# A written-out order of 2,640 steps in a transformer kernel, replaced by another order of the same steps

## The chip, the core and the metric

The kernel runs on one core of a Trainium2 chip. Its time is the time of one execution on the device, in microseconds (us). A profile is one execution recorded by the hardware profiler. Its engines are TensorE (PE, with weight loads shown apart as PEld), VectorE (DVE), ScalarE (ACT), GpSimd (POOL) and SyncE (SP), which here only issues transfers (DMAs). Each engine works through its own list of instructions in order, and waits on semaphores for what the others produce.

## The reference

For 16 batch elements of 256 tokens with 256 features, in float32: an attention of x to a context y with RMS norms (layer 0), then a decoder block on its result: causal self-attention with rotary embedding (layer 1), cross-attention to the same y with rotary embedding (layer 2), and an MLP with 1,024 hidden features. Every attention has 16 heads of 16 features. Cut to what matters:

```python
# layer 0
Q = rmsnorm(x) @ Wq; K = rmsnorm(y) @ Wk; V = rmsnorm(y) @ Wv
x = rmsnorm(x + softmax(Q K^T * scale) V @ Wo)
# layer 1
h = ln(x); q, k, v = h @ sa_wq, h @ sa_wk, h @ sa_wv
x = x + causal_attention(rope(q), rope(k), v) @ sa_wo
# layer 2
h = ln(x); q, k, v = h @ ca_wq, y @ ca_wk, y @ ca_wv
x = x + attention(rope(q), rope(k), v) @ ca_wo
# MLP
x = x + gelu(ln(x) @ fc1_w) @ fc2_w
```

## The kernel before, in words

There are 48 attentions, 16 batch elements in each of three layers. ORDER gives the layer of each of the 48 in the order in which they run; the number of an attention (0 to 47) is its place there. Class Att holds the parts of one attention as methods, and most of them are generators: each `yield` ends a segment whose instructions go to one engine (or to one engine's DMA queue). PLAN, a long string written out by hand, says in which order the segments of all attentions are called: each word, such as `q.18` or `scores.16.2`, runs the next segment of that generator (`step`). The instructions are issued in just this order, so PLAN fixes the order on every engine and in every queue. The MLP follows in a loop of its own; only a few words `mlp...` at the end of PLAN belong to it.

The methods, and what their segments are, in the order of the work:

- `stats_x`, `stats_y` (mean squares on VectorE, then the root on GpSimd, L525 and L526), `send` and `receive` (a row of roots through DRAM) for layer 0. `stats`, `norm` (L553, VectorE) for layers 1 and 2. The normed tile is turned either by TensorE (`turn`, copied by ScalarE, L575) or by VectorE in 32 by 32 pieces (`pieces`, L584) and a way through DRAM: the second segment of `pieces` stores (L592, `turn_hop<-bits`), `pieces_in` reads back (L598).
- `q`, `k`, `v`: a dense group of 16 matrix products on TensorE (L633 or L645), then the segments that take it out of PSUM: for layers 1 and 2 a bias addition on ScalarE (L760), a shuffle and two products on VectorE (L768, L774), their sum (L810, L863, L866). `q_high`, `q_low`, `k_high`, `k_low` split the result into two parts for a faster kind of product in layers 0 and 2 (from attention 2 on); `q_out` and `k_out` move them between partitions by DMA (L840, L887).
- `scores.i.n`: block n of the scores of attention i on TensorE (L964 for the fast kind, L953 for the other), then two exponentials on ScalarE (L976), and in layer 1 two masks on GpSimd (L984). `values.i.n`: the product with v (L1007); halfway ScalarE copies the result out (L1022), at the end `take_last` does so on VectorE.
- `heads_in`, `sums_in`, `invert`, `divide`: DMAs (L1030, L1041, L1054, L1060) and VectorE work (L1051, L1067) that divide by the sums. `project`: the output product (L645) and the residual addition (L1080). `finish` ends layer 0. `keep` adds a bias row to the residual on GpSimd (L621).
- `combine`: eight additions and subtractions on GpSimd (L1124, L1135) that prepare sums of weights for the MLP. `load_piece`, `load_later`: loads issued by GpSimd; `load_early`: by SyncE.

Tiles come from pools with few buffers; a segment that takes a tile waits until a former user of that buffer is done. The ones that matter here: the tag `a` (two buffers) holds the biased q or k until its rotation is done, and also the pieces ("bits") until they are stored; `hl` has one buffer, `qm`, `kT` and `av` have two; the PSUM tiles of scores have two sets, the dense ones three, the values one.

Of the kernel before, what the change touches and what calls it, by code (L numbers as in the profile page):

```python
# [54 lines left out]
scores.0.0 scores.0.0 v.0 scores.0.0 scores.0.1 q.1 scores.0.1 scores.0.1 spread.1 spread.1  # L55
scores.0.2 q.1 v.1 v.1 v.0 scores.0.2 v.0 scores.0.2 stats_x.3 values.0.0 values.0.1 stats_x.2
stats_x.3 scores.0.3 v.1 values.0.1 load_piece.5.0 k.1 stats_x.2 scores.0.3 send.2 stats_y.2
scores.0.3 k.2 send.2 k.1 load_piece.5.1
scores.1.0 load_early.4 k_high.2 load_early.0 k_low.2 q.2 scores.1.0 send.3 receive.2 scores.1.0
values.0.2 load_early.3 send.3 scores.1.1 q.3 scores.1.1 q.2 scores.1.1 values.0.3 k_out.2  # L60
q_high.2 scores.1.2 take_last.0 q_low.2 v.2 v.2 stats_y.2 scores.1.2 receive.3 q_low.2 stats_y.3
scores.1.2 q_out.2 values.1.0 stats_y.6 load_piece.6.1 scores.1.3 sums_in.0 stats_y.3 stats_x.6
k.3 scores.1.3 scores.1.3 load.4 values.1.1 k_high.3
scores.2.0 values.1.1 k_low.3 scores.2.0 values.1.2 q.3 invert.0 values.1.3 scores.2.0 heads_in.0
take_last.1 q_high.3 scores.2.1 invert.0 v.3 k_out.3 q_low.3 scores.2.1 q_low.3 heads_in.0
scores.2.1 v.2 stats_x.4 q_out.3 scores.2.2 k.4 stats_x.4 stats_y.4 sums_in.1 scores.2.2
load_piece.5.2 send.4 scores.2.2 values.2.0 v.3 send.4 divide.0 v.3 k_high.4 scores.2.3 q.4
load_early.2 scores.2.3 invert.0 invert.1 k_low.4 scores.2.3 divide.1 values.2.1 stats_y.4
receive.4 invert.1
scores.3.0 heads_in.1 values.2.1 stats_x.6 fold_of_att scores.3.0 heads_in.1 load_piece.5.3  # L70
values.2.2 divide.0 scores.3.0 q.4 values.2.3 k_out.4 q_high.4 scores.3.1 take_last.2 project.0
q_low.4 scores.3.1 invert.1 q_low.4 scores.3.1 values.3.0 q_out.4 project.0 fold_of_att scores.3.2
project.0 v.4 v.4 load_piece.6.0 scores.3.2 stats_y.8 project.0 scores.3.2 values.3.1 sums_in.2
finish.0 scores.3.3 values.3.1 stats.5 k.6 fold_of_att scores.3.3 v.4 stats.5 scores.3.3
values.3.2 load_later.0 norm.5 k_high.6 divide.1 load_piece.6.2
scores.4.0 heads_in.2 stats_x.8 values.3.3 scores.4.0 turn.5 send.6 send.6 take_last.3 scores.4.0
project.1 fold_of_att fold_of_att turn.5 heads_in.2 k_low.6 scores.4.1 invert.2 project.1 q.5
sums_in.3 scores.4.1 fold_of_att load_early.1 scores.4.1 receive.6 values.4.0 project.1 heads_in.3
q.5 scores.4.2 invert.3 k.5 project.1 invert.2 q.5 scores.4.2 q.5 load_later.1 invert.3 scores.4.2
q.5 values.4.1 load_piece.7.1 q.5 k.5 load_piece.7.0 scores.4.3 q.5 invert.2 values.4.1  # L80
load_piece.7.2 q.6 k.5 q.5 stats_y.6 k.5 scores.4.3 k.5 heads_in.3 v.5 v.5 scores.4.3 divide.2 k.5
load_piece.6.3 q.6 stats_x.8 values.4.2 invert.3 v.5 q_high.6
scores.5.0 divide.3 finish.1 q_low.6 k_out.6 values.4.3 scores.5.0 v.6 take_last.4 scores.5.0
scores.5.0 stats.7 sums_in.4 scores.5.1 divide.2 stats.7 q_low.6 project.2 v.6 scores.5.1 norm.7
scores.5.0 pieces.7 q_out.6 scores.5.1 scores.5.1 values.5.0 project.2 pieces.7 scores.5.2
project.2 scores.5.1 heads_in.4 k.8 send.8 invert.4 scores.5.2 project.2 divide.3 invert.4
scores.5.2 v.6 scores.5.2 values.5.1 finish.2 keep.5 k_high.8
scores.6.0 values.5.1 stats.9 pieces_in.7 project.3 scores.6.0 scores.5.2 k_low.8 stats.9
scores.6.0 values.5.2 heads_in.4 divide.4 norm.9 stats_y.8 project.3 scores.6.1 take_last.5
load_later.9 q.7 scores.6.1 project.3 sums_in.5 load_later.8 scores.6.1 pieces.9 heads_in.5  # L90
values.6.0 stats_y.10 q.7 scores.6.2 pieces.9 k.7 q.7 send.8 scores.6.2 invert.5 q.7 invert.5
scores.6.2 invert.4 q.7 values.6.1 q.7 scores.6.3 receive.8 q.7 k.7 q.8 invert.5 q.7 k.7
values.6.1 pieces_in.9 v.7 v.7 k.7 scores.6.3 load_later.4 k.7 load_piece.7.3 scores.6.3 k.7
heads_in.5 values.6.2 divide.5 q.8 project.3
scores.7.0 divide.4 q_high.8 v.7 k_out.8 project.4 scores.7.0 stats_x.10 scores.7.0 scores.7.0
values.6.3 heads_in.6 load_later.5 scores.7.1 divide.5 scores.7.0 take_last.6 project.5 project.4
scores.7.1 q_low.8 scores.7.1 scores.7.1 q_low.8 v.8 project.5 q_out.8 scores.7.1 stats.11
scores.7.2 sums_in.6 project.4 stats.11 q.9 scores.7.2 load_later.7 norm.11 scores.7.2 finish.3
scores.7.2 values.7.0 heads_in.6 pieces.11 stats_x.10 q.9 values.7.1
scores.8.0 load_piece.8.0 q.9 values.7.1 k.10 pieces.11 scores.7.2 scores.8.0 q.9 v.8 load_later.6  # L100
scores.8.0 send.10 values.7.2 v.8 send.10 stats_y.10 gain_ca k_high.10 q.9 scores.8.1 project.4
k.9 q.9 scores.8.1 keep.7 pieces_in.11 take_last.7 invert.6 scores.8.1 values.8.0 stats_x.14 k.9
invert.6 scores.8.2 q.9 v.9 v.9 k.9 load_piece.9.0 scores.8.2 k_low.10 divide.6 sums_in.7
load_piece.8.1 scores.8.2 k.9 values.8.1 keep.9 k.9 q.9 scores.8.3 values.8.1 invert.6 k.11 v.9
scores.8.3 k.9 heads_in.7 scores.8.3 finish.4 values.8.2 invert.7 receive.10 k.11 heads_in.7
scores.9.0 k.11 values.8.3 invert.7 scores.9.0 k.11 k_out.10 q.10 take_last.8 scores.9.0
scores.9.0 k.11 load_later.10 sums_in.8 scores.9.1 q.10 scores.9.0 stats.13 stats_x.14 q_high.10
v.10 divide.6 v.10 scores.9.1 divide.7 q_low.10 invert.7 stats.13 project.6 scores.9.1 q_low.10
scores.9.1 v.10 q_out.10 scores.9.2 project.6 scores.9.1 heads_in.8 invert.8 q.11 k.11 scores.9.2
load_piece.8.2 heads_in.8 divide.7 scores.9.2 load_piece.9.1 values.9.0 send.14 project.6  # L110
scores.9.2 q.11 invert.8 values.9.1 scores.9.2 k_high.11
scores.10.0 q.11 load_later.3 values.9.1 project.7 norm.13 scores.10.0 k_low.11 scores.10.0 q.11
values.9.2 k_out.11 pieces.13 q.11 scores.10.1 project.7 k.12 scores.10.1 take_last.9 q.11
scores.10.1 invert.8 values.10.0 stats.12 q_high.11 pieces.13 scores.10.2 stats.12 sums_in.9 v.11
q_low.11 scores.10.2 divide.8 norm.12 load_piece.10.0 k.12 heads_in.9 q_low.11 v.11 turn.12
scores.10.2 k.12 values.10.1 q_out.11 stats.16 turn.12 scores.10.3 pieces_in.13 values.10.1 v.11
fold_of_fc1 stats.16 scores.10.3 divide.8 q.12 load_later.2 k.12 scores.10.3 k.12 load_piece.8.3
k.12 values.10.2 q.12 stats_y.14
scores.11.0 fold_of_fc1 k_high.12 project.8 fold_of_fc1 invert.9 scores.11.0 stats_y.14 norm.16
heads_in.9 q.12 scores.11.0 project.6 values.10.3 k_low.12 invert.9 q.12 scores.11.1 q.12 k_out.12  # L120
k.13 scores.11.1 take_last.10 q.12 scores.11.1 heads_in.10 values.11.0 q_high.12 scores.11.2
invert.9 v.12 v.12 divide.9 q_low.12 scores.11.2 keep.11 send.14 q_low.12 scores.11.2 project.8
values.11.1 q_out.12 gain_fc1.0 k.13 scores.11.3 divide.9 k.14 sums_in.10 scores.11.3 v.12
scores.11.3 project.9 pieces.16 keep.12 values.11.1 k.13 k_high.14
scores.12.0 k.13 project.9 values.11.2 scores.12.0 k.13 pieces.16 values.11.3 heads_in.10 stats.15
scores.12.0 take_last.11 heads_in.11 stats.15 scores.12.1 k.13 q.13 receive.14 norm.15 scores.12.1
sums_in.11 invert.10 scores.12.1 k_low.14 divide.10 values.12.0 project.8 invert.10 q.13
scores.12.2 heads_in.11 q.13 values.12.1 scores.12.2 pieces_in.16 q.13 v.13 v.13 scores.12.2 q.13
q.13 values.12.1 invert.10 scores.12.3 q.13 q.13 pieces.15 q.14 scores.12.3 v.13 pieces.15
scores.12.3 k_out.14 values.12.2 q.14  # L130
scores.13.0 divide.10 fold_of_fc1 finish.6 k.15 scores.13.0 pieces_in.15 stats.19 scores.13.0
stats_x.17 scores.13.0 values.12.3 q_high.14 scores.13.1 take_last.12 k.15 invert.11 v.14 v.14
# [216 lines left out]
def xattn_kernel(  # L349
# [1068 lines left out]
    combined = []  # L1418
# [77 lines left out]
    def begin(word):  # L1496
# [3 lines left out]
        if name == "combine":  # L1500
            return combine()
        args = [int(a) for a in args]
# [562 lines left out]
```

## Time and profile before

| | us |
|---|---|
| median of 3 runs (lowest, highest) | 887.47 (886.6, 888.52) |
| the profiled execution's own time | 891.12 |
| its span, first to last instruction | 889.4 |
| TensorE busy | 871.2 |
| VectorE busy | 690.9 |
| ScalarE busy | 570.4 |
| GpSimd busy | 349.3 |

The page gives the busy time of each engine, the span in 40 equal slices (a digit is the busy share in tenths; PEclk is TensorE's granted clock in tenths of full speed), the DMA queues, the chain of waits that ended last and the costliest groups of instructions. A line of the timeline reads: start, length, engine, source line, operation, what it writes and what it reads, shapes, how many instructions, and in brackets the idle time before with what ended it. A TensorE group of 16 matrix products in float32 appears as 32 instructions.

### The profile page before, as it was taken

The numbers are of one execution on the slowest core, as the hardware profiler recorded it, in microseconds if no ns is written. First come the engines' busy times: TensorE is split into PE (matmuls) and PEld (weight loads), VectorE is DVE, ScalarE is ACT, GpSimd is POOL, SyncE is SP. The second block draws the span as 40 slices with busy tenths as digits, with TensorE's granted clock in tenths as the row PEclk, the third lists the DMA queues.
The fourth block names the chain that finished last, engine by engine and source line by source line (L and its number), as shares of the span: only waits on it lengthen the run. The fifth ranks groups of instructions, "written<-read, shape, count | busy, mean of one in ns | idle before, by whom it ended". The sixth has DMA issues, their size and how long they took to land.

```text
span 889.4 us, 32873 instructions
## 1 busy us (share of the span) xinstructions
PE 871.2 (98%) x13762; PEld 559.2 (63%) x13762; DVE 690.9 (78%) x1534; ACT 570.4 (64%) x801; POOL 349.3 (39%) x558
## 2 busy tenths in 40 slices
PE   8999999999999999999999999999999999999997
PEld 4455555555555555555554555555556799999997
DVE  5468789888888889889885888989894677777662
ACT  4787567776686767778756777777875733334440
POOL 3234766517364246175483335345142132221000
PEclk9999999999999999999999999999999999999999
DMA  8666455544444344343434233233431022111201
GB/s 273 208 193 176 147 163 175 178 132 133 134 148 123 110 134 161 117 159 120 155 118 145 84 124 111 87 118 116 158 107 54 17 72 72 57 44 44 72 25 50
DMA packets 101454, 107.04 MB, mean 120 GB/s; under 512 B 26602, under 2 KB 81778, under 8 KB 101298
## 3 DMA queue, kind: packets, MB, share of 16 engines
q1 hardware_dynamic: 96210, 89.89, 30.7%
q0 software_dynamic: 4400, 14.42, 5.7%
q8 instruction: 110, 1.80, 0.9%
q10 hardware_dynamic: 688, 0.54, 0.2%
q14 instruction: 46, 0.38, 0.1%
HBM read 46.33 MB, written 13.65 MB: 67 GB/s over the span
## 4 chain that ended last, share of the span: by engine, by line
PE 79%; DVE 8%; DMA 5%; ACT 2%; issue 2%; SPq 2%; POOL 2%; ACTq 0%; DVEq 0%; POOLq 0%
PE d L633 15%; PE d L645 14%; PE A L1007 14%; PE S L964 7%; PE upX L1221 6%; PE A L1319 6%; PE S L953 5%; PE downZ L1319 3%; PE upZ L1221 3%; PE d L1319 2%; PE d L1221 2%; ACT pt L976 1%; DMA turn_hop<-bits 1%; DMA qm<-qm 1%; DVE xn L553 1%
## 5 line engine op out<-in xcount | busy, mean ns | idle before, releaser
L976 ACT ACTIVATE pt<-S 128x1024 f32<-128x1024 f32 x224 | 217.7, 1023 | 98.9 <-PE S L953 59.4
L1007 PE MATMUL A<-pt,va 128*32 128x256 f32 (+1 forms) x3072 | 184.6, 363 | 2.9 <-ACT av L1022 2.7
L976 ACT ACTIVATE pt<-S,sy 128x1024 f32<-128x1024 f32 x128 | 136.4, 1115 | 35.5 <-PE S L964 26.2
L1007 PEld LDWEIGHTS A<-pt,va 128*32 128x32 f32 x3072 | 94.1, 110 | 68.0 <-issue 7.0
L984 POOL TENSOR_SCALAR_AFFINE_SELECT pt<-pt 128x512 f32<-128x512 f32 x128 | 90.7, 728 | 74.4 <-ACT pt L976 73.9
L964 PEld LDWEIGHTS S<-qm,kT 32*128 32x128 f32 x1920 | 66.9, 183 | 52.2 <-issue 24.2
L964 PE MATMUL S<-qm,kT 32*128 32x256 f32 x1920 | 93.5, 304 | 3.8 <-ACT pt L976 3.4
L621 POOL TENSOR_TENSOR cur<-cur,bias 128x512 f32<-128x512 f32 x48 | 64.8, 1353 | 32.9 <-DVE xn L553 32.7
L525 POOL TENSOR_SCALAR r_ln<-bmv 128x2 f32<-128x2 f32 x48 | 14.4, 300 | 149.6 <-DVE bmv L544 137.4
L953 PE MATMUL S<-qm,kT 32*64 32x512 f32 (+1 forms) x1152 | 63.3, 512 | 1.1 <-DVE kT L866 1.0
L760 ACT ACTIVATE a<-d,qk_bias 128x256 f32<-128x256 f32 x128 | 53.9, 477 | 14.0 <-PE d L633 4.8
L1243 ACT COPY g<-upX 128x512 f32<-128x512 f32 x28 | 15.0, 589 | 72.4 <-issue 68.1
L633 PE MATMUL d<-hT,sa 128*32 128x256 f32 x1024 | 61.4, 382 | 0.0
L553 DVE TENSOR_SCALAR xn<-cur,bmv,r_ln 128x256 f32<-128x256 f32 x96 | 47.5, 543 | 4.2 <-POOL r_ln L526 4.0
L1067 DVE TENSOR_TENSOR oT<-oT,inv 128x512 f32<-128x512 f32 x48 | 38.2, 798 | 15.1 <-DMA rq<-rq_hop 3.7
L774 DVE TENSOR_TENSOR a<-a,turn 128x512 f32<-128x512 f32 x64 | 47.9, 748 | 1.3
L1259 ACT ACTIVATE g<-g,fb 128x256 f32<-128x256 f32 x96 | 41.0, 499 | 11.1 <-DVE g L1248 11.1
L768 DVE STREAM_SHUFFLE u<-a 128x512 f32<-128x512 f32 x64 | 47.5, 743 | 0.4 <-issue 0.4
L774 DVE TENSOR_TENSOR u<-u,turn 128x512 f32<-128x512 f32 x64 | 47.0, 734 | 0.0
L1065 POOL TENSOR_TENSOR seen<-seen,sums 128x64 f32<-128x64 f32 x48 | 20.9, 436 | 62.9 <-DVE sums L1051 59.2
L633 PEld LDWEIGHTS d<-hT,sa 128*32 128x32 f32 x1024 | 30.3, 109 | 24.2 <-issue 3.2
L1022 DVE COPY av<-A 128x512 f32<-128x512 f32 x47 | 32.1, 683 | 13.4 <-PE A L1007 13.4
(176 smaller groups left out, 1701.1 us busy)
## 6 DMA issues: line engine op xcount, KB each, us to landing
kT<-hl SPq DMA_DIRECT2D x60, 256.0 KB
qm<-qm SPq DMA_DIRECT2D x60, 256.0 KB
oT<-av SPq DMA_DIRECT2D x192, 64.0 KB
inv<-inv_hop SPq DMA_DIRECT2D x96, 128.0 KB
turn_hop<-bits SPq DMA_DIRECT2D x33, 256.0 KB
hT<-turn_hop SPq DMA_DIRECT2D x92, 64.0 KB
out<-res SPq DMA_DIRECT2D x15, 256.0 KB
cur<-in_x POOLq DMA_DIRECT2D x11, 256.0 KB, 3.3
```

What stands on the lines that cost most here:

```text
L553: nc.vector.tensor_scalar(xn[:, c, :], src[:, c, :], mv[:, c, 0:1], r[:, c : c + 1], ALU.subtract, ALU.mult,)
L621: nc.gpsimd.tensor_tensor(t, t, bias_sb[:, row : row + D].unsqueeze(1).to_broadcast([P, NC, D]), ALU.add)
L633: nc.tensor.matmul(o, lhsT=w[:, k, at + t * P + j : at + t * P + j + 32], rhs=tokens, start=(k == 0), stop=(k == KC - 1), skip_group_check ...
L645: nc.tensor.matmul(ps[j : j + 32, c * D : (c + 1) * D], lhsT=some_tokens(src, k, c, j), rhs=w[:, k, at : at + D], start=(k == 0), stop=(k ...
L774: nc.vector.tensor_tensor(t, t, table.unsqueeze(1).to_broadcast([P, KC, S]), ALU.mult)
L953: nc.tensor.matmul(ps[64 * half : 64 * half + 64, 2 * m * u : 2 * m * (u + 1)] .rearrange("p (i s) -> p i s", i=2), lhsT=self.kT[r, t, at] ...
L964: nc.tensor.matmul(ps[:, at : at + m], lhsT=self.kd[r, i, t, kc * P : (kc + 1) * P].bitcast(F32R), rhs=self.qd[r, i, h, t, q0:S].bitcast(F ...
L976: nc.scalar.activation(pt[:, :, :w], ps[:, :, :w], AF.Exp, scale=scale)
L984: nc.gpsimd.affine_select(out=diag, in_=diag, compare_op=ALU.is_ge, fill=0.0, base=0, pattern=[[0, 2], [0, 2], [1, P]], channel_multiplier=-1,
L1007: nc.tensor.matmul(self.av[32 * r : 32 * r + 32, i, q0:S], lhsT=self.va[:, kc, 8 * t + 2 * r + i, :], rhs=pts[r // 2][:, r % 2, i * m : (i ...
L1221: nc.tensor.matmul(o if len(b.shape) == 2 else by_groups(o), lhsT=a[:, c * P : (c + 1) * P], rhs=b, start=(first and c % 2 == 0), stop=Tru ...
L1319: nc.tensor.matmul(ps[:, c, :], lhsT=a[f // 2][:, f % 2, c * P : (c + 1) * P], rhs=b[:, f, :], start=(first and c == 0 and f == 0), stop=True,
```

## The change

PLAN is replaced by another order of the same words. `combine` is changed with it: its word's number now chooses between the two generators, where the number was not read before. The PLAN's diff covers nearly all of its lines; here are the places that the prediction speaks of, and the whole change of code:

```diff
...
-load_later.9 q.7 scores.6.1 project.3 sums_in.5 load_later.8 scores.6.1 pieces.9 heads_in.5
-values.6.0 stats_y.10 q.7 scores.6.2 pieces.9 k.7 q.7 send.8 scores.6.2 invert.5 q.7 invert.5
...
-values.15.1 q.16 scores.15.3 invert.14 pieces.19 q.17 scores.15.3 q.16 pieces.19 stats_x.20
-k_out.17 values.15.1 project.13 q.16 project.12 stats_x.20 scores.15.3 q.17 values.15.2 q_high.17
...
-scores.32.0 invert.30 k.33 stats.37 divide.29 values.31.2 invert.30 scores.32.0 norm.35 keep.33
-k.33 send.36 v.33 scores.32.0 k.33 combine.0 take_last.31 scores.32.1 invert.30 norm.37
-load_piece.14.3 q.33 scores.32.1 pieces.35 v.33 divide.30 stats.39 k.33 sums_in.31 scores.32.1
-values.32.0 k.33 combine.2 pieces.35 scores.32.2 q.33 heads_in.30 project.29 keep.37 scores.32.2
...
-scores.46.0 q.47 divide.44 values.45.3 scores.46.0 q.47 project.44 scores.46.0 q.47 q.47 k_high.47
-scores.46.1 q.47 v.47 v.47 take_last.45 scores.46.1 k_low.47 sums_in.45 scores.46.1 mlp.1.stats
-values.46.0 q_high.47 scores.46.2 k_out.47 project.43 q_low.47 scores.46.2 q_low.47 scores.46.2
-mlp.0.norm values.46.1 q_out.47 scores.46.3 invert.45 project.44 invert.45 divide.45 scores.46.3
-mlp.0.keep v.47 mlp.0.turn project.43 heads_in.45 values.46.1 scores.46.3 mlp.0.turn values.46.2
...
+scores.6.1 take_last.5 norm.9 scores.6.1 sums_in.5 values.6.0 pieces.9 q.7 values.6.1 project.3
+pieces.9 invert.4 scores.6.2 q.7 values.6.1 k.7 scores.6.2 q.7 receive.8 load_early.2 invert.5
...
+sums_in.15 k.18 scores.16.1 turn.18 pieces.21 invert.14 scores.16.2 turn.18 send.20 keep.18 v.17
+q.18 pieces.21 scores.16.2 k.18 scores.16.1 scores.16.2 invert.15 stats_y.20 values.16.0 invert.15
+scores.16.2 q.18
...
+scores.31.0 take_last.30 scores.31.0 q_low.32 combine.0 scores.31.1 finish.27 scores.31.0
...
+scores.32.0 values.31.1 invert.30 divide.29 k.33 invert.30 keep.33 values.31.2 scores.32.0 k.33
+send.36 load_piece.14.3 v.33 scores.32.0 k.33 send.34 v.33 take_last.31 stats.35 k.33 invert.30
+scores.32.1 combine.1 k.33 q.33 scores.32.1 stats.39 receive.34 stats.37 scores.32.1 sums_in.31
+values.32.0 divide.30 v.33 q.33 stats_y.34 scores.32.2 norm.35 project.29 scores.32.2 pieces.35
...
+scores.33.0 keep.35 pieces.37 invert.31 k.34 q_low.34 scores.33.0 receive.36 project.30
...
+scores.33.1 values.33.0 k.35 scores.33.2 combine.2 k.35 heads_in.32 project.31 invert.32
...
+values.33.2 pieces_in.37 keep.37 v.34 q.35 scores.34.1 take_last.33 v.35 v.35 combine.4
...
+scores.46.1 k_low.47 values.46.0 divide.44 q_high.47 k_out.47 scores.46.2 values.46.1 q_low.47
+scores.46.2 q_low.47 project.44 scores.46.2 v.47 q_out.47 invert.45 divide.43 invert.45
+scores.46.3 project.44 project.43 scores.46.3 mlp.0.norm values.46.1 scores.46.3 mlp.1.stats
+mlp.0.keep values.46.2 heads_in.45
...
-    def combine():
+    def combine(n):
...
-            combined.extend([*[combine_down()] * 4, *[combine_up()] * 4])
-        next(combined.pop(0))
+            combined.extend([combine_down(), combine_up()])
+        next(combined[n // 4])
...
-            return combine()
+            return combine(int(args[0]))
```

## The prediction

> **What bounds the kernel now.** I read the page's first two parts, then who TensorE waits for, then TensorE's own instructions in order of time.
>
> ```profile
> span 889.4 us, 32873 instructions
> ...
> PE 871.2 (98%) x13762; PEld 559.2 (63%) x13762; DVE 690.9 (78%) x1534; ACT 570.4 (64%) x801; POOL 349.3 (39%) x558
> ...
> PEclk9999999999999999999999999999999999999999
> ```
>
> TensorE is the bound: busy for 98% of the span, at full clock. An order changes no TensorE work, so it can win only what TensorE loses between groups. To size that I took from the timeline the usual time from one group's start to the next one's: 1.75 us for a dense group (lines 633, 645), 0.89 for a values group (L1007), 0.68 for a fast scores group (L964), 1.05 for a slow one (L953), 0.58 for a transposed tile, 0.09 more for whatever comes ahead of scores. What each group takes beyond this is lost. Within the PLAN (10.5 to 683.4 us in the trace) the excesses add up to 20.0 us, in these places: start 1.4; 97 to 114 us 3.1; 205 to 252 us 2.7; 362 to 376 us 1.2; 441 to 472 us 5.5; 553 us 0.8; the end, 665 to 676 us, 3.4; others, each under 0.4, 2.0. So 20.0 us (2.2%) is the ceiling. The worst place:
>
> ```profile
> 466.31 1.05 PE L1007 MATMUL A<-pt,va 128*32 128x256 f32 x16
> 468.83 0.38 PE L964 MATMUL S<-qm,kT 32*128 32x256 f32 x2 [1.48 <-ACT pt L976]
> 469.84 0.90 PE L964 MATMUL S<-qm,kT 32*128 32x256 f32 x14 [0.62 <-ACT pt L976]
> 470.67 3.39 PE L633 MATMUL d<-xT,w 128*32 128x256 f32 x32
> ```
>
> TensorE idles 1.48 and 0.62 us for ScalarE's exponentials, and then a dense group takes 3.39 us where 1.93 is usual: 1.46 us more, with 0.91 granted in that 20 us stretch. Why ScalarE was late stands in the other engines' timeline:
>
> ```profile
> 458.04 1.27 POOL L621 TENSOR_TENSOR cur<-cur,bias 128x512 f32<-128x512 f32 x1
> 458.06 2.69 DVE L553 TENSOR_SCALAR xn<-cur,bmv,r_ln 128x256 f32<-128x256 f32 x2
> 459.28 1.33 POOL L1124 TENSOR_TENSOR down_t<-fc 128x512 f32<-128x512 f32 x1
> ...
> 464.54 1.73 POOL L621 TENSOR_TENSOR cur<-cur,bias 128x512 f32<-128x512 f32 x1
> ...
> 465.16 1.66 DVE L866 TENSOR_TENSOR kT<-a,u 128x512 f32<-128x512 f32 x1
> 466.93 0.84 ACT L760 ACTIVATE a<-d,qk_bias 128x256 f32<-128x256 f32 x2 [3.48 <-DVE kT L866]
> ```
>
> Beside GpSimd's large additions VectorE's pair of L553 takes 2.69 us; four microseconds later the same pair takes 0.73. VectorE falls behind, and ScalarE, first in first out, holds at a bias addition that needs a tile which VectorE has still to free; the exponentials stand behind it. The other type of loss, at 97 to 114 us:
>
> ```profile
> 104.74 0.52 SPq L592 DMA_DIRECT2D turn_hop<-bits  x1
> ...
> 109.88 0.84 ACT L760 ACTIVATE a<-d,qk_bias 128x256 f32<-128x256 f32 x2 [3.96 <-DMA turn_hop<-bits]
> ```
>
> The tile of k.7 is the one that pieces.9 is still being stored from: the store took 5.04 us (in the chain of waits; others there took 2.03, 2.01 and 2.75), and ScalarE lost 3.96 us.
>
> **The change part by part.** It removes and adds no instruction: both PLANs hold the same 2,640 words, each as often. combine's number now says whether a down (0 to 3) or an up step (4 to 7) comes next, where four down steps came first; the same eight additions, 0 us. What is left is order, and I compared the two orders by TensorE time: each word gets as its place the sum of the usual group times ahead of it, from 12 us on, to 664 in both.
>
> *Crowded stretches.* I gave each word its engines' mean durations from the cost groups, and summed them over stretches of 20 us of TensorE time (neighbours overlap by about a tenth, so the sums only compare). VectorE's fullest stretches go from 23.9, 22.4 and 22.2 us to 21.7, 21.2 and 21.1; for the stretches at 80, 440 and 540, where time was lost, 21.1 to 19.7, 21.3 to 19.7, 22.4 to 19.8. GpSimd's go from 16.1 to 11.0 at 80 and from 16.3 to 12.2 at 440. In particular keep.33, combine.0, combine.2 and keep.37, which stood within 7.7 us of TensorE time (448.6 to 456.3), now stand at 447.3, 439.4, 470.9 and 478.8, with combine.1 and keep.35 at 451.1 and 463.4.
>
> *Distances of transfers.* Least TensorE time between a transfer's issue and who needs it, before and after: store of the pieces to its reading back 1.99, 3.41; reading back to the q that uses it 3.41, 4.64 (median 16); q_out to the scores 2.24, 3.10 (median 4.27, 5.09); k_out to the next writer of its one tile 3.41, 5.70; heads_in to the copy that reuses its tile 3.41, 5.16; a q to the transfer that overwrites its row 1.75, 3.74. Worse: pieces store to the next taker of its tile, under 4 us in 7 places for 6, and 0.89 us at least for 1.75 (pieces.21 ahead of q.18; the old one, pieces.19 ahead of q.17, lies in the 2.7 us at 205 to 252); receive to q 2.55 for 2.74; a scores group to its values group within 0.5 us of what must lie between (two exponentials, 1.94 us, and for the causal ones a mask) in 11 places for 4; and SyncE, which issues all these transfers, has 18.4 us of issue time in its fullest stretch where it had 16.6. The loads by GpSimd keep at least 4.3 us to their first user (5.1 before) and land in 3.3 to 4.7: priced at nothing, and the VectorE statistics behind them would pay if they came later.
>
> *Price by place.* At 97 to 114 us k.7's distance grows from 3.41 to 4.27, VectorE and GpSimd are eased: I take two thirds, −2.1. At 441 to 472 us the additions are apart: −4.5 of 5.5 (1.0 left, since heads_in.28 still stands 5.16 ahead of its copy, which cost 0.61 at 441.6). At 553 us −0.7. At 205 to 252 us nothing: VectorE's 23.9 + 18.5 become 21.1 + 21.2. At 362 to 376 us nothing, the load there is as before. At the end, project.43 and project.44 now stand between values.46.1 and values.46.2, whose copy cost 1.13, and the first scores of the last two attentions lie 0.57 further apart: −1.7; the wait behind mlp.0.up2's copies stays. Sum −9.0. New losses: 1.1 at q.18, behind whose bias addition ScalarE has the exponentials of scores.16.2 and TensorE the groups that wait for those (a store of 2.01 against 0.89); 0.3 for the two shortest other stores (2.55 and 2.64 against 2.75); 0.8 for seven more close values (7 at the usual 0.12 of the small excesses): +2.2. Net −6.8 in the profiled execution. Bounds: nothing regained (+2.2), or all but the start and the copies of mlp.0.up2 (1.4 and 1.5), −17.
>
> That execution took 891.12 us for its span of 889.4; the runs' median is 887.47, 3.65 less, so part of its 20.0 us is accident: typical runs lose about 16.4, 0.82 of it. −6.8 × 0.82 = −5.6, and **887.5 − 5.6 = 881.9 us**.
>
> *Two rules weighed.* VectorE's 2.69 us beside GpSimd's 1.27 and 1.33. The Trainium skill, SBUF — State Buffer, "SBUF: two separate sides", says that the two engines' shared ports are locked for a whole instruction and the loser stands still. By it the same 48 additions block as long wherever they stand, so the 4.5 us would turn up elsewhere: 881.9 + 4.5 × 0.82 = 885.6. I stay with the rows, since most of VectorE's delays meet TensorE busy and only heaped ones reach it.
> The slow dense group followed 2.1 us of idle time within 3.5 us. TensorE: Matmul & The Clock Gate, "HAM oscillation", names idle gaps over about 3.4 us as what lowers the clock. By it the 1.46 us belong to no gap of this order and would not leave with it: 1.2 us less gained, 883.1. The row shows them right behind the gaps, so I count them.
>
> **The rivals.** *Nearly all is regained.* For it: every listed transfer but two has more room, no stretch is over 21.7. Against: the margins between scores, exponentials and values, which a 98% busy engine feels first, are no wider. −17 × 0.82 = −14: 873.5.
> *Nothing is regained.* VectorE's and GpSimd's totals stay, each delay comes out elsewhere, as the 205 to 252 us place suggests: 887.5.
> *Slower: the piece tiles.* ScalarE holds at a tile whose store runs, exponentials behind it, as at 104.74. That place cost 2.6 us (1.32, 0.84, 0.19 and 0.24 beyond the usual); all seven places under 4 us at this price are 18.2, against 9.0 regained: +9.2 × 0.82, 895. It decides from 1.3 us per place on (9.0 over 7): the seven stand 2.8 us apart on average, so the stores would have to take about 4 us, where three of the four rows show 2.0 to 2.75. Midway between that point (887.5) and the full price lies 891.
> *That the change doesn't do what it says* is hardly open: every word is there as often as before, and the tables above show that they moved.
>
> **How the numbers follow.** About 0.2% (1.8 us) is what a measurement of this kernel can tell from no change. Forecast (partly regained, 875 to 885.6) 0.43; nearly all (about 873.5) 0.17; nothing (885.7 to 889.2) 0.14; slower (from 889.3) 0.26. So faster 0.60, same 0.14, slower 0.26. Range 873.5 to 891: it leaves out half of the nearly-all case and half of the slower one. The likeliest case's own range is 875 to 885.6.
>
> **What would show it.** Right: no TensorE wait over 1 us near 450 to 475 us, VectorE's pairs of L553 there near 0.7 us, granted clock 1.00 in every stretch, ScalarE's wait for the store of the pieces under 2 us, the first upX nearer to 677 us than to 683.4. Wrong: waits on L760 for turn_hop in several places, or new TensorE waits for L976 or L1022 where values stand close behind their scores; or TensorE's groups slower with no wait at all, which no place in an order would explain.

## The result, and the profile after

The new order takes 884.73 us (median of 11 runs, 883.27 to 887.85) where the old one, run in turn with it on the same chip, takes 888.21 (11 runs, 884.86 to 890.05): ratio 0.9965, 95% interval 0.9949 to 0.9982. That is 0.35% faster. The forecast was 0.63% (881.9 for 887.47): the sign was right, the size about half of what was predicted, though 884.73 lies in the range. The profiled execution of the new order took 883.68 us, its span is 881.9.

From here on a ratio is always to the kernel before, run in turn on the same chip, with its 95% interval. Line numbers shift with PLAN's length: what is L553 before is L549 after, and one less than that in most experiments.

The page after, its busy times and the granted clock:

```profile
span 881.9 us, 32904 instructions
...
PE 867.6 (98%) x13762; PEld 559.8 (63%) x13762; DVE 686.7 (78%) x1534; ACT 569.1 (65%) x801; POOL 347.2 (39%) x558
...
PEclk9999999999999999999999999999999999999999
```

The place that was worst is mended. VectorE and GpSimd after, from the timeline:

```profile
457.57 1.30 POOL L1120 TENSOR_TENSOR down_t<-fc,down_t 128x512 f32<-128x512 f32 x1
459.30 0.73 DVE L549 TENSOR_SCALAR xn<-cur,bmv,r_ln 128x256 f32<-128x256 f32 x2
```

The pair takes 0.73 us (2.69 before), because GpSimd's addition has ended ahead of it (so does the next pair, at 467.98), and TensorE has no wait between 440 and 480 us. So is the place at 97 to 114 us: ScalarE's bias additions there wait for no store. But there is a new loss, where the old order had none. TensorE, VectorE and SyncE in the timeline after:

```profile
53.89 0.33 SPq L720 DMA_DIRECT2D rq<-rq_hop  x1
54.35 1.36 SPq L1056 DMA_DIRECT2D inv<-inv_hop  x2
...
56.99 1.23 PE L960 MATMUL S<-qm,kT 32*128 32x256 f32 x16
57.58 0.69 DVE L790 TENSOR_TENSOR qa<-d,rq 128x512 f32<-128x512 f32 x1 [4.96 <-DMA rq<-rq_hop]
58.18 0.68 DVE L1018 COPY av<-A 128x512 f32<-128x512 f32 x1
59.01 1.07 PE L1003 MATMUL A<-pt,va 128*32 128x256 f32 x16 [0.79 <-DVE av L1018]
61.91 0.69 DVE L1063 TENSOR_TENSOR oT<-oT,inv 128x512 f32<-128x512 f32 x1 [3.04 <-DMA inv<-inv_hop]
62.65 2.92 PE L641 MATMUL d<-w0o,oT 128*32 128x256 f32 x32 [2.57 <-DVE oT L1063]
```

VectorE stands 4.96 us at q.4's product (L790) until its row of roots has come. Behind it in VectorE's list is take_last.2 (L1018), which empties the one PSUM tile of values, and TensorE waits for that. Then VectorE waits for the row of inverse sums, and TensorE for project.0's input. The dense group behind this takes 2.92 us where 1.93 is usual, with 0.91 granted from 60 to 80 us. The same place before:

```profile
55.81 0.69 DVE L1067 TENSOR_TENSOR oT<-oT,inv 128x512 f32<-128x512 f32 x1 [3.66 <-DMA rq<-rq_hop]
56.93 0.69 DVE L794 TENSOR_TENSOR qa<-d,rq 128x512 f32<-128x512 f32 x1 [0.43 <-DMA rq<-rq_hop]
57.79 0.74 PE L964 MATMUL S<-qm,kT 32*128 32x256 f32 x16
57.93 0.69 DVE L1022 COPY av<-A 128x512 f32<-128x512 f32 x1 [0.31 <-PE A L1007]
58.47 1.93 PE L645 MATMUL d<-w0o,oT 128*32 128x256 f32 x32
60.22 1.05 PE L1007 MATMUL A<-pt,va 128*32 128x256 f32 x16
```

VectorE waits here too, but the inverse sums come first (SyncE issued them from 51.80 us, ahead of the row), the row is there when the copy is due (VectorE then waits 0.31 us for TensorE, not TensorE for it), and project.0 covers the copy. What TensorE loses, summed from the timeline as in the prediction (all excesses now, also the small and the negative ones, from the start to 690 us, where the usual group times are good to some tenths), is this. Before is the mean of four profiles (the first, and three that the experiments below add), after that of five of the new order (after, a1, e2, e6, e8; e2 moves three words of the end and e6 and e8 three words near 450 us, which changed their places by 0.7 us at most):

| place, us | before | lowest, highest | after | lowest, highest | forecast of the change |
|---|---|---|---|---|---|
| 45 to 75 | 0.5 | 0.5, 0.5 | 5.5 | 4.2, 6.8 | 0 |
| 75 to 120 | 3.1 | 2.9, 3.3 | -0.1 | -0.2, 0.1 | -2.1 |
| 200 to 258 | 2.9 | 1.9, 4.0 | 0.8 | 0.4, 1.1 | +1.1 (q.18) |
| 358 to 380 | 1.0 | 0.7, 1.1 | 0.2 | -0.2, 0.4 | 0 |
| 436 to 480 | 4.1 | 0.8, 5.7 | -0.3 | -0.7, 0.0 | -4.5 |
| 545 to 560 | 0.4 | 0.0, 0.8 | 0.4 | 0.4, 0.4 | -0.7 |
| 660 to 690 | 4.1 | 3.9, 4.3 | 4.1 | 4.0, 4.2 | -1.7 |
| rest | 4.6 | 4.1, 4.8 | 5.3 | 4.3, 5.8 | +1.1 |
| sum | 20.6 | 17.3, 23.1 | 15.9 | 14.8, 17.1 | -6.8 |

### The profile page after: what moved, and what is told of

Same layout as the page of the kernel before. It is cut to its first block, busy times and chain, and to the rows that moved or that the text cites. A ratio compares the mean times of both kernels' runs of the same rounds, so it can differ in the third digit from the quotient of the medians.

```text
span 881.9 us, 32904 instructions
## 1 busy us (share of the span) xinstructions
PE 867.6 (98%) x13762; PEld 559.8 (63%) x13762; DVE 686.7 (78%) x1534; ACT 569.1 (65%) x801; POOL 347.2 (39%) x558
## 4 chain that ended last, share of the span: by engine, by line
PE 93%; DMA 2%; DVE 1%; SPq 1%; ACT 1%; issue 1%; POOL 0%; ACTq 0%; POOLq 0%; DVEq 0%
PE d L641 19%; PE d L629 19%; PE A L1003 17%; PE S L960 9%; PE S L949 7%; PE upX L1217 6%; PE A L1315 6%; PE downZ L1315 3%; PE upZ L1217 3%; PE d L1315 2%; PE d L1217 2%; DMA inv<-inv_hop 1%; PE d L564 1%; PE downX L1315 1%; ACT pt L972 1%
## 5 line engine op out<-in xcount | busy, mean ns | idle before, releaser
L1003 PE MATMUL A<-pt,va 128*32 128x256 f32 (+1 forms) x3072 | 182.2, 363 | 1.3 <-DVE av L1018 0.8
L521 POOL TENSOR_SCALAR r_ln<-bmv 128x2 f32<-128x2 f32 x48 | 15.2, 318 | 136.3 <-DVE bmv L540 135.3
L549 DVE TENSOR_SCALAR xn<-cur,bmv,r_ln 128x256 f32<-128x256 f32 x96 | 51.9, 591 | 1.7 <-POOL r_ln L522 1.7
L1061 POOL TENSOR_TENSOR seen<-seen,sums 128x64 f32<-128x64 f32 x48 | 18.7, 389 | 86.4 <-DVE sums L1047 70.5
L1018 DVE COPY av<-A 128x512 f32<-128x512 f32 x47 | 32.2, 684 | 20.9 <-PE A L1003 20.7
L770 DVE TENSOR_TENSOR a<-a,turn 128x512 f32<-128x512 f32 x64 | 45.3, 707 | 1.7
L1310 DVE TENSOR_TENSOR g<-g,g 128x512 f32<-128x512 f32 x64 | 40.6, 682 | 0.0
```

The costliest lines, as they stand in the source:

```text
L770: nc.vector.tensor_tensor(t, t, table.unsqueeze(1).to_broadcast([P, KC, S]), ALU.mult)
L1003: nc.tensor.matmul(self.av[32 * r : 32 * r + 32, i, q0:S], lhsT=self.va[:, kc, 8 * t + 2 * r + i, :], rhs=pts[r // 2][:, r % 2, i * m : (i ...
```

## The experiments

In four sets, each on one chip: a1 to e3, e4 to e7, then b1 and e8 to e10, at last b2, b3 and e11. The kernel before had medians of 888.55, 888.27, 886.80 and 887.93 us in these sets.

**a1: the new order once more.**

> The changed kernel itself, once more, as the measure for the three runs beside it. Theory (the profiles of one execution each overstate the difference: 7.5 us between them, 3.5 us between the medians): the ratio to the kernel before lies at 0.996 to 0.997, and the profile again shows TensorE losing 4 to 6 us at 50 to 70 us and 3 to 4 us at 660 to 680 us. Rival (those two places are accidents of the one execution that was profiled): the losses stand elsewhere, under 2 us at each of the two places.

884.74 us, ratio 0.9962 (0.9942 to 0.9982). The loss at 45 to 75 us is there again (4.2 us; VectorE stood 6.30 us at q.4's product), and so is the end's (4.0). Both belong to the order.

**e1: the inverse sums of attention 0 earlier.** invert.0's second segment moved 30 words ahead, its third 7:

```diff
-scores.2.1 k_out.3 ... k_low.4 invert.0 fold_of_att heads_in.1 scores.2.3 ... receive.4 invert.0
+scores.2.1 invert.0 k_out.3 ... k_low.4 fold_of_att heads_in.1 invert.0 scores.2.3 ... receive.4
```

> The changed kernel with two words moved: the second segment of invert.0 (its store to DRAM) 6.8 us of TensorE time earlier, its third (the read back) 1.5 us earlier. Theory (project.0 waits 2.57 us because the store was issued late and the read back then met four loads): the wait at 62 us goes, with the slow clock behind it, and the time falls by 3 to 5 us against the changed kernel. Rival (the read back is slow because of the four loads and the queue, wherever the store stands): under 1 us gained, the wait of project.0 stays over 1.5 us.

884.47 us, ratio 0.996 (0.994 to 0.998): nothing gained. The wait for project.0's input goes, and the wait at the values grows from 0.8 to 3.8 us. VectorE in the timeline of e1:

```profile
60.68 0.69 DVE L789 TENSOR_TENSOR qa<-d,rq 128x512 f32<-128x512 f32 x1 [8.00 <-DMA rq<-rq_hop]
61.29 0.68 DVE L1017 COPY av<-A 128x512 f32<-128x512 f32 x1
```

SyncE issues the row of roots 2.1 us later than in the profile after (56.02 for 53.89), since invert.0's transfers now stand ahead of it in its queue. So the late inverse sums are not the cause by themselves: once they are early, the copy behind the waiting product costs TensorE as much.

**e2 and e3: the end.** In e2 keep.45, keep.46 and keep.47 stand 10 to 50 us of TensorE time earlier, away from VectorE's norms of the MLP; e3 is e1 and e2 together, with mlp.0.mix ahead of the last values group as well.

> The changed kernel with keep.45, keep.46 and keep.47 moved from the last 11 us of the order to 600, 610 and 642 us of TensorE time, where GpSimd has little to do. Theory (GpSimd's additions stretch VectorE's work at the end, four of L549 from about 1.5 to 3.29 us and two of L1212 from 0.42 to 1.49 us, and upX waits 1.15 us for it): those durations fall to 1.5 and 0.5, upX waits under 0.3 us, and 1 to 1.5 us are gained. Rival (the end is bound by ScalarE's exponentials behind the copies of mlp.0.up2): the VectorE durations fall, but the time stays within 0.5 us.

885.88 us, ratio 0.9976 (0.9954 to 0.9997); 4.1 us lost from 660 to 690 us, as in the new order. The additions were not what the end loses.

> Both moves together, and mlp.0.mix moved from the end of the order to the place that it had before (656 us of TensorE time). Theory: the gains of the two runs beside it add up, 4 to 6.5 us below the changed kernel, 878.5 to 881 if that stands at 884.7. Rival (the first takes over what the other frees, since a delay at 60 us only shifts everything behind it): no more than the better of the two.

883.79 us, ratio 0.9951 (0.993 to 0.9973), not told apart from the new order's. The wait of 1.15 us for VectorE's g goes, and another of 0.9 us takes its place; 3.7 us are lost there. Part of what holds the end came out in e11.

**e4: VectorE's queue.** e1, and q.4's waiting segment behind what TensorE needs:

```diff
-values.2.3 q.4 k_out.4 scores.3.0 take_last.2 q_high.4 scores.3.1 divide.0 invert.1 values.3.0
-q_low.4 scores.3.1 project.0 q_low.4 scores.3.1
+values.2.3 k_out.4 scores.3.0 take_last.2 scores.3.1 divide.0 q.4 invert.1 values.3.0
+scores.3.1 q_high.4 q_low.4 project.0 q_low.4 scores.3.1
```

> The order after, with invert.0's last segments early (as in e1_inv0) and three words of attention 4 later: q.4's second segment behind divide.0's second (it stood ahead of take_last.2), q_high.4 and q_low.4 behind scores.3.1. So VectorE's copy of attention 2's last values no longer stands behind a product that waits for the row of roots (4.96 to 8.00 us of VectorE waiting at that product in the five profiles of this order so far). Theory (a wait of VectorE's queue that stands ahead of what TensorE needs): TensorE's waits for the copy av and for oT both go, what TensorE loses between 50 and 70 us falls from 3.7 to 6.9 us to under 1.5, and the median falls by 3 to 4 us to about 881.3, 0.992 of the kernel before. Rival (the row is late whatever stands behind it, and the loss only moves, to q_out.4 and the first scores of attention 4): the loss between 50 and 85 us stays at 3.5 us or more, median about 884.6, ratio 0.996.

880.96 us, ratio 0.9926 (0.99 to 0.9952): the theory's number. VectorE and TensorE in the timeline of e4:

```profile
57.61 0.69 DVE L1017 COPY av<-A 128x512 f32<-128x512 f32 x1 [4.52 <-PE A L1002]
58.64 1.07 PE L1002 MATMUL A<-pt,va 128*32 128x256 f32 x16
59.85 0.69 DVE L1062 TENSOR_TENSOR oT<-oT,inv 128x512 f32<-128x512 f32 x1 [1.54 <-DMA inv<-inv_hop]
60.59 1.93 PE L640 MATMUL d<-w0o,oT 128*32 128x256 f32 x32 [0.89 <-DVE oT L1062]
60.94 0.69 DVE L789 TENSOR_TENSOR qa<-d,rq 128x512 f32<-128x512 f32 x1 [0.41 <-DMA rq<-rq_hop]
```

The row is as late as in e1 (60.94 for 60.68), but the copy no longer stands behind it, and the values group starts with no wait. The loss from 45 to 75 us is 2.9 (it was to be under 1.5): 0.9 for the inverse sums remain, and 0.9 at exponentials that stand behind q_high.4 on ScalarE. The wait did not move to attention 4. No run moves q.4's segment without the inverse sums, so e4 shows the worth of the two together, and e1 that the sums alone give nothing.

**e5: the additions, in the old order.** Three words moved in the order before, nothing else:

```diff
-q_low.32 receive.34 ... k.33 combine.0 take_last.31 ... k.33 combine.2 pieces.35 ... project.29 keep.37 scores.32.2
+q_low.32 combine.0 receive.34 ... k.33 take_last.31 ... k.33 pieces.35 ... project.29 scores.32.2
-scores.33.2 scores.33.1 ... stats.41 v.34
+scores.33.2 combine.2 scores.33.1 ... stats.41 keep.37 v.34
```

> The order before with three words moved and nothing else: combine.0 some 11 us of TensorE time earlier, combine.2 some 17 later, keep.37 some 22 later, as the new order has them, so that keep.33 is left of the four large GpSimd additions of 448 to 456 us. Theory (these additions beside VectorE's statistics make VectorE late, ScalarE holds and TensorE waits): the loss from 441 to 472 us, 5.5 us in the profile, falls under 1.5 us, no pair of L553 there is over 1 us, and the median falls by 2.5 to 4.5 us, to about 885, ratio 0.996; the group of runs at 889 to 891 us should be gone. Rival (an addition costs VectorE as much wherever it stands): the loss turns up elsewhere, median 888.5, ratio 1.000. The other old places (97 to 114 and 205 to 252 us) are untouched, so this profile also shows how often they recur: if the profile of before was typical, 3.1 and 2.7 us again.

885.24 us, ratio 0.9972 (0.9956 to 0.9989), and no run over 887.75. The place at 436 to 480 us loses 1.2. VectorE in the timeline of e5, against 2.69 us for the pair and 466.82 us for the end of kT in the first profile of before:

```profile
457.71 0.80 DVE L548 TENSOR_SCALAR xn<-cur,bmv,r_ln 128x256 f32<-128x256 f32 x2
...
462.43 0.69 DVE L861 TENSOR_TENSOR kT<-a,u 128x512 f32<-128x512 f32 x1
```

Three words out of 2,640 give 3.0 us by the medians (2.5 by the ratio), nearly as much as the whole change gave net. The delay did not come out elsewhere: the other places hold 15.2 us, for 16.5 in the mean of before. The rule that the prediction weighed (the Trainium skill, SBUF — State Buffer, "SBUF: two separate sides") is right in that additions on GpSimd hold VectorE up (the pair takes 2.69 us beside them, 0.73 without); what the prediction drew from it, that 4.5 us would turn up elsewhere, is not what this run shows.

**e6: additions put back into the new order.** combine.0 behind k.33's fourth segment, combine.1 ahead of stats.37's first, combine.2 ahead of norm.35.

> The order after with combine.0, combine.1 and combine.2 put back beside keep.33 and around norm.35, so that four large GpSimd additions stand within some 9 us of TensorE time ahead of and beside VectorE's norm of attention 35. Theory of the heap: that norm's pair of L549 takes over 2 us where it takes 0.73, TensorE waits over 1 us for exponentials between 450 and 475 us, and the median rises by 2.5 to 4.5 us to about 888, ratio 1.000. Rival (the old place was made by its close distances, kT and the exponentials, and not by the additions): no wait there over 0.5 us, median 884.7, ratio 0.996.

885.27 us, ratio 0.9968 (0.9953 to 0.9984), no wait there. But the additions ended at 458.45 and 462.77 us and the norm's pair began at 462.51 (0.74 us): only 0.26 us of them stood beside it, so this run decides nothing about additions beside a norm. e8 does it better. What e6 does show is a product three instructions ahead of kT in VectorE's list: it took 2.32 us for 0.69 (from 456.69) beside the first of these additions, and TensorE lost nothing by it.

**e7: the loads.** load_piece.6.1, 7.1 and 5.2 moved behind stats_x.8's second segment, stats_y.8 behind stats.5's, so that the row of roots travels beside one load and not up to four.

> The order after with three of the four loads that GpSimd issues between 54 and 59 us moved behind GpSimd's next computation (issued near 67 us), and the statistics that read one of them moved behind those of attention 5. The row of roots for q.4 then travels beside one load. Rival to the theory of e4_q4 (the loads stretch the row's transfer): the row lands 2.4 us after its issue, as in the profile of before, where it took 3.7 to 4.8 us in the profiles of this order, VectorE's wait at the product falls under 3 us, TensorE's wait for av goes, and the median falls to about 882, ratio 0.993. Theory of the queue alone (the row's way is as long without the loads): VectorE still waits 5 us or more there, the loss from 50 to 70 us stays at 3.7 or more, median 884.7, ratio 0.996.

883.13 us, ratio 0.9959 (0.9938 to 0.9981), not told apart from the new order's 0.9962. VectorE still waits 5.01 us at the product, and the loss from 45 to 75 us is 4.0. The row took 3.61 us from its issue (54.45) to the product's start (58.06), where it took 3.7 to 4.8 in the new order's other profiles: the loads cost it 0.1 to 1.2 us, and the loss stands without them. The expectation's "2.4 us in the profile of before" was a misreading: that wait is labelled with the row, but it is the one of the sums' product, and the row's own product starts at 56.93, 3.56 us after the row's issue (53.37). The rival falls.

**b1, b2, b3: the kernel before, three more profiles.**

> The kernel before once more, for a second profile of it. The forecast took 18% of the losses in the first profile (20.0 us, of an execution of 891.12 us) for accident, evenly over the places. If the losses are fixed by the order, the places show 3.5 us at 90 to 120 us, 2.8 at 200 to 258 and 5.7 at 436 to 480 again, summed from the timeline by the usual group times. If they scatter from execution to execution, one of them, most likely the one at 436 to 480 us, comes out 2 us or more smaller and the execution is nearer to 888 us. Rival: they all come out smaller by the same share.

> A third profile of the kernel before. In the first the place at 436 to 480 us lost 5.7 us, in the second 0.8, and the executions took 891.12 and 885.87 us; every other place came out within 0.6 us of the first. If that place is what makes the kernel before scatter, a third execution shows either about 5 us there and a time near 890, or about 1 us and a time near 886, with all other places as before. Rival (the two differ in this place by chance, and other places move as much in other executions): another place differs by 2 us or more.

> A fourth profile of the kernel before, with the same two readings as the third. All four together give a first idea of how often the place at 436 to 480 us is lost: the runs' median fell by 3.0 us when the additions were spread (e5_before_spread), which by 5 us a time would be some 6 executions in 10.

885.87, 888.63 and 891.32 us (the first profile: 891.12). The place at 436 to 480 us lost 0.8, 4.2 and 5.7 us (first: 5.7), that at 200 to 258 us 3.1, 1.9 and 4.0 (2.8); all others agree within 0.8 us. So one place makes most of the scatter, and a second some of it. VectorE and GpSimd in the second profile of before (b1), where the place was nearly free:

```profile
457.61 0.72 DVE L553 TENSOR_SCALAR xn<-cur,bmv,r_ln 128x256 f32<-128x256 f32 x2
458.24 1.27 POOL L621 TENSOR_TENSOR cur<-cur,bias 128x512 f32<-128x512 f32 x1
...
459.48 1.72 POOL L1124 TENSOR_TENSOR down_t<-fc 128x512 f32<-128x512 f32 x1
...
463.33 0.69 DVE L866 TENSOR_TENSOR kT<-a,u 128x512 f32<-128x512 f32 x1
```

The pair started 0.45 us earlier than in the first profile (458.06) and 0.63 us ahead of the first addition, where there the two started together (458.04). So it took 0.72 us for 2.69, kT was done at 464.02 and not at 466.82, and TensorE did not wait for exponentials. In b2 and b3 the additions caught it (2.07 and 2.70). A loss of 5 us hangs on half a microsecond.

**e8: additions beside the norm, in the new order.** combine.1 and combine.2 behind stats.39's second segment, combine.0 behind stats_y.34's.

> The order after with three of GpSimd's large additions (combine.1, combine.2, combine.0) put directly behind one another so that two of them run while VectorE does the norm of attention 35 (in e6_after_heap they ran 1 to 4 us ahead of it and nothing was to be seen). If additions beside VectorE's product are what slows it, the pair of L548 for attention 35 takes over 2 us again, 0.73 in the order after, and VectorE is 1.5 to 3 us later behind it. What that costs TensorE: by the theory that any heap reaches it 2 to 4 us (median about 887.5, ratio 0.999); by the rival that only a heap ahead of an operation that ScalarE or TensorE waits for soon (kT and k's shuffles in the order before) reaches it, under 1 us (median 885, ratio 0.996).

884.52 us, ratio 0.9983 (0.9964 to 1.0003; the median of before is the lowest of the four here, and by its own median this run is the new order's). GpSimd and VectorE in the timeline of e8:

```profile
458.05 0.69 DVE L861 TENSOR_TENSOR kT<-a,u 128x512 f32<-128x512 f32 x1
...
459.28 1.29 POOL L1119 TENSOR_TENSOR down_t<-fc 128x512 f32<-128x512 f32 x1
...
460.31 1.77 DVE L548 TENSOR_SCALAR xn<-cur,bmv,r_ln 128x256 f32<-128x256 f32 x2
460.65 1.28 POOL L1119 TENSOR_TENSOR down_t<-fc,down_t 128x512 f32<-128x512 f32 x1
```

The pair takes 1.77 us beside the additions (over 2 was expected), and a product behind it 1.82 for 0.69, some 2 us together; TensorE loses nothing from 436 to 480 us (-0.1). kT, which ScalarE and TensorE wait for, stands ahead of the norm here; in the order before it stands behind. That agrees with the second reading, that a heap costs when what is waited for soon is queued behind it. It does not show it: the two orders differ here in more than kT's place, and in e6 a stretched product ahead of kT cost nothing.

**e9: the early part undone.** The old order up to the first scores of attention 5 (84 us of TensorE time), the new one from there.

> The order before up to the first scores of attention 5 (84 us of TensorE time), and from there the order after: the early part of the change is undone, with its close row of roots, and the rest kept. Theory (the new loss at 50 to 70 us is what the forecast missed, and the rest gave what it promised): the loss from 45 to 75 us is 0.5 us as in the profile of before, for 4.0 to 6.9 in the profiles of the order after, and the median is 3.5 to 5 us under that of the order after, 880 to 881, ratio 0.991 to 0.992. Rival (the total is fixed by other things, and an early loss is regained later): median 884.7, ratio 0.996.

879.26 us, ratio 0.9931 (0.9904 to 0.9957). The loss from 45 to 75 us is 0.5, the rest as after; 10.7 us are lost in all. This is the change without the loss that the forecast did not see: 0.9931 of 887.47 is 881.3, and the forecast was 881.9. The agreement is in part luck, since the parts of the sum are others than those forecast (see below).

**e10: the place at 97 to 114 us alone.** The old order, with the words from the first scores of attention 5 to those of attention 11 in the new order. (`combine` has the new code, by which its fourth and fifth step change places here.)

> The order before, in which only the words from the first scores of attention 5 to the first scores of attention 11 (84 to 166 us of TensorE time) stand as in the order after. It asks what the place at 97 to 114 us is worth by itself. Forecast's reading: the loss there falls from 3.5 us (two profiles of that order) to 0.3 (all profiles of the order after), and the median by 2 to 3.5 us to 885 to 886, ratio 0.997. Rival (the delay there is made good later, or appears in one execution in two): under 1 us, ratio 0.999 or more.

883.95 us, ratio 0.9967 (0.9948 to 0.9987): 2.85 us of median. The loss from 75 to 120 us is -0.2 for 3.1. The line that answers to ScalarE's wait of 3.96 us, from the timeline of the order after:

```profile
106.40 0.83 ACT L756 ACTIVATE a<-d,qk_bias 128x256 f32<-128x256 f32 x2
```

**e11: e9 with another end.** To e2's moves and e3's move of mlp.0.mix comes one more: mlp.0.up2, whose two copies ScalarE made ahead of the exponentials of scores.47.1, behind them.

```diff
-scores.47.1 mlp.1.stats mlp.0.turn mlp.0.up2 sums_in.46 scores.47.1 heads_in.46 scores.47.1
+scores.47.1 mlp.1.stats mlp.0.turn sums_in.46 scores.47.1 mlp.0.mix heads_in.46 scores.47.1 mlp.0.up2
```

> e9_head (the order before up to 84 us of TensorE time, then the order after) with the end changed: keep.45, keep.46 and keep.47 10 to 50 us earlier, mlp.0.mix ahead of the last values, and mlp.0.up2 behind both exponentials of scores.47.1 in place of ahead of them. The forecast counted 1.7 us of gain at the end that did not come (3.9 us lost there in the profile of before, 3.7 to 4.2 in those of the order after): the exponentials wait behind ScalarE's two copies of mlp.0.up2. If that is the cause, the loss from 660 to 690 us falls from 3.9 to about 2.5 and the wait of scores.47.2 for its exponentials goes, median 878 to 879, ratio 0.990 to 0.991. Rival (those exponentials would be late anyway, since TensorE has little else to do there): no change, 879.3, ratio 0.992.

877.21 us (876.4 to 878.79), ratio 0.9893 (0.9863 to 0.9922): the fastest of all. ScalarE and TensorE at the end of e9:

```profile
660.20 0.59 ACT L1239 COPY g<-d 128x512 f32<-128x512 f32 x1 [0.28 <-PE d L1217]
660.69 1.95 ACT L972 ACTIVATE pt<-S 128x1024 f32<-128x1024 f32 x2
661.77 0.38 PE L960 MATMUL S<-qm,kT 32*128 32x256 f32 x2 [0.60 <-ACT pt L972]
```

And of e11:

```profile
658.55 1.94 ACT L972 ACTIVATE pt<-S 128x1024 f32<-128x1024 f32 x2 [0.91 <-PE S L960]
660.37 1.08 ACT L1239 COPY g<-d 128x512 f32<-128x512 f32 x2
661.31 0.75 PE L960 MATMUL S<-qm,kT 32*128 32x256 f32 x16
```

In e9 ScalarE waits 1.92 us for TensorE's dense group (to 659.34), copies twice, and only then starts exponentials whose scores were ready (the scores group ran from 657.50 to 658.25). In e11 they start at 658.55, and the next scores group has no wait. The loss from 660 to 690 us falls from 3.9 to 2.0. The other moves without this one left 4.1 (e2) and 3.7 us (e3) there, so most of it is the copies' place.

## Why the prediction was right in sign and wrong in size

**The bound and the ceiling** held. TensorE is busy 98% in both orders, and all differences of time are differences of what TensorE loses between groups: the profiled sums fell from 22.3 to 14.9 us, the spans by 7.5.

**97 to 114 us** (-2.1 forecast): the mechanism was right, the gain was all of it, 3.1 us; by itself it gave 2.85 us of median (e10).

**441 to 472 us** (-4.5): right in mechanism; e5 shows it by moving three words. The size was taken from one profile in which the place lost 5.7 us. The mean of four is 4.1, and its worth in medians is 3.0 (e5). The step that failed here is the scaling, "−6.8 × 0.82", as if the accident in that execution were spread evenly over the places. It sat mostly in this place: the three steady places (45 to 75, 75 to 120, 660 to 690) differ by at most 0.4 us over four profiles, this one by 4.9. The error in size stayed small here: -4.5 × 0.82 is -3.7, where e5 gave 3.0 and the means of the profiles give 4.4.

**205 to 252 and 362 to 376 us** (0): 2.1 and 0.8 us were gained. VectorE's fullest stretch there was eased, and the prediction did not trust that. No run tells which of the moved words did it. At the second place it is not even shown that the order did: project's group, which waits there for VectorE (0.55 us at 373.68 in the first profile of before), has no wait in e10, whose words there are the old ones.

**553 us and the end** (-0.7, -1.7): at 553 us the loss was an accident of the first profile. A dense group is 0.77 us late there; in the other three profiles of before none is late at this place. At the end both gains came, and a wait that the prediction had at nothing took most of them back. TensorE before and after:

```profile
667.17 1.07 PE L1007 MATMUL A<-pt,va 128*32 128x256 f32 x16 [1.06 <-ACT av L1022]
```

```profile
679.35 1.99 PE L1217 MATMUL upX<-ts,up_s 128*128 128x256 f32 x8 [1.15 <-DVE g L1244]
```

The wait for the copy of values.46.1 is gone, and so are the 0.57 us at the scores group behind it; new is the wait for VectorE's g. From the first upX to the end of the span the four profiles of before take 206.0 us (683.42 to 889.4 in the first), the new order's 207.4 (674.48 to 881.9). The wait behind mlp.0.up2's copies stayed, as forecast; moving the copies is what mended it (e11).

**New losses foreseen** (+2.2): at q.18 ScalarE waits 1.19 us for the store of pieces.21, just as priced (1.1), but the place loses at most 1.1 us in all, for 2.9 before. The other short stores and close values show no wait. The rival of the piece tiles fell: apart from those 1.19 us ScalarE waits for no store.

**The new loss not foreseen** (5.0 us at 45 to 75) is the step that failed and decided the size: the prediction's new losses, +2.2 in all, have no term for it. "Receive to q 2.55 for 2.74" was listed among the worse distances and then given no price, and no distance was taken for the inverse sums. The 0.19 us were not the point. In both orders q.4's product stands ahead of take_last.2 in VectorE's list, and its row comes about when that copy is due. What changed is the cover. The TensorE time between attention 2's last values group and attention 3's first one went from 2.52 to 0.77 us, the least of all 47 such gaps in either order (all others are 1.75 or more), a distance that the table did not have; and the transfers of attention 0's inverse sums are issued 2.55 us later (54.35 for 51.80), behind the row, with the sums' product and project.0 waiting for them. They also took longer, 7.6 us from issue to use (to 61.91) for 4.0 (to 55.81); why is open. So VectorE's waits became TensorE's. How the loss divides between the short cover and the late sums is not shown, since no run changes the cover alone. e4 mends about half of it (5.5 to 2.9 us in the profiles) by changing what stands behind what, with the gap still 0.77; e9 mends it by undoing the early part. Against the new order's median (884.74) they are 3.8 and 5.5 us faster, by the ratios (0.9926 and 0.9931 for 0.9963) 3.3 and 2.8; the profiles give 2.6 and 5.0 for the place.

The sum thus reads: about -10.5 us in the places from 75 to 690 us of the table, where -7.9 was forecast (-9.0, and +1.1 at q.18), +5.0 at one place forecast at nothing, and +0.7 for the rest, where +1.1 was forecast. By the means of four and five profiles that is -4.7 us; the runs' medians say -3.5 to -3.8. The one pair of profiles, 7.5 us apart, would have made the forecast look right for the wrong reason.

## What to carry to other kernels

When an order written by hand is compared with another, list for each engine what stands *behind* an instruction that waits for a DMA, and price it by who needs that next; a wait that TensorE did not feel in one order cost it 5 us in the other, where 0.77 us of work for 2.52 lay ahead of what it needed next. Size what a place loses from several profiles, since a place that hangs on two engines meeting within half a microsecond loses 0.8 us in one execution and 5.7 in the next, while others never change. Two orders that agree about their state at some point can be spliced there, which tells in one run which part holds a gain or a loss, and here gave the better kernel.

## What the runs showed of the hardware beyond this

The clock fell after gaps of about 2 us, but not after all of them. At 460 to 480 us of the order before, gaps of 1.17 and 0.63 us, 0.38 us of work apart (1.80 together, b2), left the granted clock at 1.00 and the next dense group at 1.93 us; gaps of 1.48 and 0.62 (2.10, the first profile) and of 1.81 and 0.62 (2.43, b3) are followed by 0.91 in that stretch, and by dense groups that took 1.46 and 1.67 us too long (in b3 over two groups). With no gap (b1) there was no slow group. So at this place the prediction's reading, that the 1.46 us belong to the gaps, agrees with the four profiles.

The length of the gaps does not decide it alone. From 60 to 80 us of e3 a single gap of 1.90 us, before the values group at 60.53, is followed by 0.91 and a dense group of 2.72 us; in a1 gaps of 2.13 and 0.85 us, 1.1 us of work apart, left 1.00 and a dense group of 1.93. What else decides it is open. The rule that the prediction weighed (the Trainium skill, TensorE: Matmul & The Clock Gate, "HAM oscillation", with gaps over about 3.4 us) does not foresee a fall after 1.90 or 2.10 us.
